# Gated cross-attention block: quantized tokens of blocks 2 to 8 transposed by DMA, with a given order behind the attention and in the first layer

## The chip, the cores and the metric

The kernel runs on one core of a Trainium2 chip. The metric is device time in microseconds of one execution. The time before is 717.9 us, the median of 3 runs (715.8 to 718.52). The profile that is read here is of one execution by itself, with a time of its own.

The engines of the core are TensorE (PE; its weight loads are listed as PEld), VectorE (DVE), ScalarE (ACT), GpSimd (POOL) and SyncE (SP), which here only issues DMAs. SBUF is the on-chip memory that all of them and the DMAs reach; PSUM is the accumulation memory that TensorE writes.

## The reference

A Flamingo-style gated block with x of 2 x 2048 tokens of 512 numbers, and 77 context tokens for each of the 2 batch entries:

```python
x = x + tanh(g_xattn) * xattn(layernorm(x), ctx, ctx, Wq, bq, Wk, bk, Wv, bv, Wo, bo)
x = x + tanh(g_ffn) * ffn(layernorm(x), w1, b1, w2, b2)

def ffn(x, w1, b1, w2, b2):               # 512 -> 2048 -> 512
    h = qlinear(x.reshape(-1, 512), w1, b1)
    h = gelu(h, approximate=False)
    return qlinear(h, w2, b2)

def qlinear(x, w, b):
    xq, sx = quant_per_tensor(x)
    wq, sw = quant_per_tensor(w)
    return (xq @ wq.T + b) * (sw * sx)

def quant_per_tensor(x):
    scale = max(max(abs(x)), 1e-6) / 127
    return round(x / scale), scale
```

The attention has 16 heads of 32. What matters is that each scale is one number for the whole tensor: no token of the first layer can be quantized before the attention is done for all tokens and the largest absolute value of the normalized x is known, and no hidden value can be quantized before the first layer is done for all tokens.

## The kernel before, in words

The 4096 tokens are cut into 8 blocks of 512 (block 1 is index i = 0 in the code, block 8 is i = 7), and a block into 4 tiles of 128 tokens. x stays in SBUF for all blocks. There are three stages.

**Attention.** For each block and each of 8 steps (a group of 4 heads, half of the tokens), TensorE computes scores, VectorE subtracts the maximum, ScalarE takes the exponential, VectorE sums and GpSimd divides; TensorE transposes the probabilities, applies V and projects (L326), and VectorE adds the result to x (L333). Afterwards `norm2_stats` and `norm2_max` compute for each tile the statistics of the second layer norm and the largest absolute value of the normalized tokens (`xmax`). For the last block these follow tile by tile. Weights are quantized on the way.

**Between attention and first layer.** Block 1's tokens are normalized on GpSimd (L529, four instructions), `scale_of` turns `xmax` into the scale `s_x` and its inverse `inv_x` on all partitions (a diagonal, one matmul by ones, a maximum), and `quantize_x` multiplies by it, rounds by adding and subtracting a large constant, and writes the integers as bf16 (`xq`). The first layer needs tokens on the free axis and features on the partitions, so TensorE transposes each tile in four pieces of 128x128 into PSUM (`px`, L553) and ScalarE copies it to `xqT` (L556).

**First layer.** For each block, four G tiles of four chunks of 128 hidden units. A chunk is four accumulating matmuls `ph <- w1q, xqT` (L583) of 128x512. Two chunks share one PSUM tile `ph` (two banks, two such tiles), each of which ScalarE turns into `G` by a Gelu (L590); VectorE takes the maximum of |G| over two chunks (L600). G tiles of the first six blocks are stored to DRAM by SyncE's queue (L611, 1 MB each); those of the last two stay in SBUF (8 buffers in all). While block i is in the matmuls, VectorE normalizes and quantizes block i + 1 (L529, L167, L168), TensorE transposes it and VectorE copies the result (L558). What each engine issues next is chosen by a scheduler that goes by priority, except where `issue_after` puts an instruction behind another one of the same engine, or `manual_schedule` keeps an engine to the order of the source.

**Second layer.** The scale of the hidden values is computed in the same way; G is quantized by ScalarE and VectorE (L636, L637), multiplied by `w2q` (L645), scaled and added to x (L659, L663) and stored. The 24 G tiles in DRAM are loaded again (L630) as buffers come free.

The bias b2 is loaded at the start, by the same queue of SyncE as x and the weights (L118).

The two loops that the change touches, as quoted below with their line numbers:

Of the kernel before, what the change touches and what calls it, by code (L numbers as in the profile page):

```python
# [15 lines left out]
P = 128  # L16
D = 512
# [25 lines left out]
def tile_flamingo_gated_block(  # L43
# [47 lines left out]
    wq_sb = awts.tile([P, KC, D], F32, name="wq_sb")  # L91
    wo_sb = awts.tile([P, KC, D], F32, name="wo_sb")
    ctx_sb = awts.tile([P, B, KC, NK], F32, name="ctx_sb")
    bv_sb = awts.tile([NK, D], F32, name="bv_sb")
    bq_sb = const.tile([P, KC], F32, name="bq_sb")
    bk_sb = const.tile([P, KC], F32, name="bk_sb")
    tg = const.tile([P, 2], F32, name="tg")
    bo_sb = const.tile([P, D], F32, name="bo_sb")
    b1_sb = const.tile([P, FC], F32, name="b1_sb")
    b2_sb = const.tile([P, D], F32, name="b2_sb")  # L100

    load_x(0, pieces=NT)
    nc.scalar.dma_start(bq_sb, bq)
# [11 lines left out]
    nc.sync.dma_start(tg[:, 1:2], g_ffn.to_broadcast([P, 1]))  # L115
    nc.sync.dma_start(bo_sb, bo.to_broadcast([P, D]))
    nc.sync.dma_start(b1_sb, b1)
    nc.sync.dma_start(b2_sb, b2.to_broadcast([P, D]))  # L118

    ident = const.tile([P, P], F32, name="ident")  # L120
    make_identity(nc, ident)
# [5 lines left out]
    nc.gpsimd.memset(mhalf, -0.5)  # L127

    w1q = const.tile([P, KC, FF], BF16, name="w1q")
    w2q = const.tile([P, FC, D], BF16, name="w2q")  # L130
    mean2 = const.tile([P, NB, NT, 2], F32, name="mean2")
    rstd2 = const.tile([P, NB, NT], F32, name="rstd2")
# [15 lines left out]
    def scale_of(maxima, name, psum, tag):  # L148
# [13 lines left out]
        nc.vector.reciprocal(inv, s)  # L162
        return s, inv

    def quantize(dst, src, inv):

        nc.vector.tensor_scalar(src, src, inv, MAGIC, ALU.mult, ALU.add)  # L167
        return nc.vector.tensor_scalar(dst, src, MAGIC, None, ALU.subtract).ins  # L168
# [3 lines left out]

    s_w, inv_w = {}, {}
    with actx:
        work = actx.enter_context(tc.tile_pool(name="work", bufs=2))
        ps_s = actx.enter_context(tc.tile_pool(name="ps_s", bufs=2, space=PSUM))
        ps_t = actx.enter_context(tc.tile_pool(name="ps_t", bufs=2, space=PSUM))
        ps_p = actx.enter_context(tc.tile_pool(name="ps_p", bufs=2, space=PSUM))

        kblk, vblk = [], []  # L180
        for b in range(B):
            kb = awts.tile([P, NG, RK], F32, name=f"kb{b}")
            nc.gpsimd.memset(kb, 0.0)
            kblk.append(kb)
            vblk.append(awts.tile([NK, D], F32, name=f"vb{b}"))

        def project_k(b, g):

# [153 lines left out]
        def norm2_max(i, t0=0, t1=NT):  # L342

            tm = small.tile([P, NT], F32, tag="tm", name=f"tm{i}_{t0}")
            for t in range(t0, t1):
                xn = work.tile([P, D], F32, tag="xn", name=f"xf{i}_{t}")
                nc.vector.tensor_scalar(
                    xn,
                    X[i][:, t, :],
                    mean2[:, i, t, 0:1],  # L350
                    rstd2[:, i, t : t + 1],
                    ALU.subtract,
                    ALU.mult,
                )
                nc.vector.tensor_reduce(
                    tm[:, t - t0 : t - t0 + 1], xn, AX.X, ALU.max, apply_absolute_value=True
                )
            k = i if t1 - t0 == NT else NB - 1 + t0
            nc.vector.tensor_reduce(xmax[:, k : k + 1], tm[:, : t1 - t0], AX.X, ALU.max)

# [65 lines left out]
        for i in range(NB):  # L428
            for s in range(2 * NG):
                last = None  # L430
                if s + 1 < 2 * NG:
                    last = softmax(i, s + 1)
                    last_product = last["POOL"]
                elif i + 1 < NB:
                    last = softmax(i + 1, 0)
                transpose_a(i, s, 0)

                if i == 0 and s < 2:
                    project_k(0, s + 2)
                if s == 0:  # L440
                    if i > 0:
                        apply_v(i - 1, NG - 1)
                    project_q(i, 1)
                if i == 0 and s == 1:
                    project_v(0)
                if i == 0 and s == 2:


                    with tc.issue_after(last["ACT"]):
                        nc.scalar.activation(tg, tg, AF.Tanh)  # L450
                    with tc.issue_after(last["POOL"]):
                        nc.gpsimd.tensor_scalar(bo_sb, bo_sb, tg[:, 0:1], None, ALU.mult)
                if s in (2, 4):
                    project_q(i, 1 + s // 2)
                    apply_v(i, s // 2 - 1)
                if s in (1, 3, 5, 6) and i > 0:
                    project_o(i - 1, (1, 3, 5, 6).index(s))
                if s == 6:
                    apply_v(i, 2)
                if i + 1 < NB:  # L460
                    if s == 3:
                        with tc.issue_after(last["DVE"]):
                            norm(i + 1)
                    if s in (5, 6):
                        for t in (2 * s - 10, 2 * s - 9):
                            transpose_x(i + 1, t)
                transpose_a(i, s, 1)
                if s == 6 and i + 1 < NB:
                    project_q(i + 1, 0)
                if i == 0 and 3 <= s < 7:  # L470
                    for b in range(1, B):
                        project_k(b, s - 3)
                        if s == 6:
                            project_v(b)
                if s == 7 and i > 0:
                    norm2_stats(i - 1)
                    norm2_max(i - 1)
                if last is not None:
                    with tc.issue_after(last["DVE"]):
                        weight_step(i, s)  # L480
                    t = s - NT if i == 0 else s // 2
                    if t >= 0 and (i == 0 or s % 2 == 0):
                        with tc.issue_after(last["POOL"]):
                            add_bias(i, t)
            if i + 2 < NB:
                load_x(i + 2)
            if i == 0:
                load_w("w1", w1_piece, range(4))
            if i == 2:
                load_w("w2", w2_piece, range(2))  # L490
# [4 lines left out]
        for t in range(NT):  # L495
            project_o(NB - 1, t)
            last = norm2_stats(NB - 1, t, t + 1)
            if t > 0:
                with tc.issue_after(last):
                    norm2_max(NB - 1, t - 1, t)  # L500
        norm2_max(NB - 1, NT - 1, NT)
    s_w1, s_w2 = s_w["w1"], s_w["w2"]


# [1 line left out]
    hidden_dram = ctx.enter_context(  # L506
        tc.tile_pool(name="hidden_dram", bufs=1, space=bass.MemoryType.DRAM)
    )

    def gtile(name):  # L510
        return gpool.tile([P, GF, TB], F32, tag="G", name=name)
# [5 lines left out]
    with ExitStack() as fctx:  # L517
# [1 line left out]
        ps_h = fctx.enter_context(  # L519
            tc.tile_pool(name="ps_h", bufs=2, space=PSUM, reuse_waits="tile")  # L520
        )
        ps_x = fctx.enter_context(
            tc.tile_pool(name="ps_x", bufs=2, space=PSUM, reuse_waits="tile")
        )

        def normalize_x(i, engine):
            xs = fwork.tile([P, NT, D], F32, tag="xs", name=f"xs{i}")
            for t in range(NT):
                engine.tensor_scalar(  # L529
                    xs[:, t, :],  # L530
                    X[i][:, t, :],
                    mean2[:, i, t, 0:1],
                    rstd2[:, i, t : t + 1],
                    ALU.subtract,
                    ALU.mult,
                )
            return xs

        def quantize_x(i, xs, n):

            xq = fwork.tile([P, NT, D], BF16, tag="xq", name=f"xq{i}")
            xqT = fwork.tile([P, KC, TB], BF16, tag="xqT", name=f"xqT{i}")
            for t0 in range(0, NT, n):
                v, vq = xs[:, t0 : t0 + n, :], xq[:, t0 : t0 + n, :]
                if n == 1 and t0 >= NT // 2:
                    nc.scalar.activation(v, v, AF.Copy, bias=MAGIC, scale=inv_x)
                    last = nc.vector.tensor_scalar(vq, v, MAGIC, None, ALU.subtract).ins
                else:
                    last = quantize(vq, v, inv_x)
                for t in range(t0, t0 + n):  # L550
                    px = ps_x.tile([P, KC, P], BF16, tag="px", name=f"px{i}_{t}")
                    for kc in range(KC):
                        nc.tensor.transpose(px[:, kc, :], xq[:, t, kc * P : (kc + 1) * P], identb)  # L553
                    dst = xqT[:, :, t * P : (t + 1) * P]
                    if n == 1:
                        nc.scalar.copy(dst, px)  # L556
                    else:
                        nc.vector.tensor_copy(dst, px)  # L558
            return xqT, last


        with tc.issue_after(last_product), tc.high_priority(offset=300):
            xs = normalize_x(0, nc.gpsimd)
        s_x, inv_x = scale_of(xmax, "x", ps_g, "pg")
        xqT, last = quantize_x(0, xs, 1)
        s1 = const.tile([P, 1], F32, name="s1")
        nc.vector.tensor_tensor(s1, s_x, s_w1, ALU.mult)
        b1s = const.tile([P, FC], F32, name="b1s")
        nc.vector.tensor_scalar(b1s, b1_sb, s1, None, ALU.mult)
        for i in range(NB):  # L570
            cur = xqT
            if i + 1 < NB:
                with tc.issue_after(last):
                    xs = normalize_x(i + 1, nc.vector)
                xqT, last = quantize_x(i + 1, xs, NT)
            for a in range(GT):
                G = gtile(f"G{i}_{a}")
                for v in range(GF // 2):
# [149 lines left out]
```

## Time and profile before

| What | us |
|---|---|
| median of 3 runs | 717.9 |
| the profiled execution's own time | 718.17 |
| its span, first to last instruction | 716.2 |
| first matmul of the first layer, after the span's start | 457.57 |
| ScalarE's last Gelu begins | 584.26 |
| first matmul of the second layer | 592.33 |

The page divides the span into 40 equal slices; a digit is the busy share in tenths (9 is 90% or more). PEclk is the clock that TensorE was granted, in tenths, DMA the busy share of 16 DMA engines:

```profile
PE   4998999899999999999999997699999978999977
PEld 2655445445445445454555543344444433444433
DVE  3564678889888799587577668799997669855542
ACT  2455344334344334444444440477777779454540
POOL 2134323234232342432333232300000009991000
PEclk9999999999999999999999999699999999999999
DMA  9900200121311311100000000066666107699871
```

One slice is 17.9 us. The attention ends in slice 25 to 26 (digit 7 and 6 of PE; the granted clock falls to 0.6 there), the first layer follows to the slice with digit 7 after the row of nines, then the second layer.

The groups of instructions that the change touches (line, engine, operation, out<-in, partitions x elements, count | busy us, mean ns of one | idle before it, and what ended it):

```profile
L583 PE MATMUL ph<-xqT,w1q 128*128 128x512 bf16 x512 | 124.2, 381 | 0.9 <-ACT xqT L556 0.7
L590 ACT ACTIVATE G<-ph,b1s,s 128x512 f32<-128x512 f32 x128 | 99.5, 777 | 28.9 <-PE ph L583 23.8
L600 DVE TENSOR_REDUCE hmax<-G 128x1 f32<-128x1024 f32 x63 | 73.9, 1213 | 16.0 <-ACT G L590 15.7
L529 DVE TENSOR_SCALAR xs<-x,mean,rstd 128x512 f32<-128x512 f32 x28 | 14.0, 540 | 0.0
L553 PE MATMUL px<-identb,xq 128*128 128x128 bf16 x128 | 11.6, 230 | 5.1 <-DVE xq L168 2.7 <-ACT xqT L556 2.4
L558 DVE COPY xqT<-px 128x512 bf16<-128x512 bf16 x28 | 10.6, 416 | 1.2 <-PE px L553 1.0
L167 DVE TENSOR_SCALAR xs<-xs,inv_x 128x2048 f32<-128x2048 f32 x7 | 9.0, 1281 | 0.1
L529 POOL TENSOR_SCALAR xs<-x,mean,rstd 128x512 f32<-128x512 f32 x4 | 8.7, 2174 | 0.0
L168 DVE TENSOR_SCALAR xq<-xs 128x2048 bf16<-128x2048 f32 x7 | 8.5, 1218 | 0.0
```

A matmul's mean (381 ns) is from its start to its end in a pipeline, so that neighbours overlap; how many fit into a time is read from when they start.

### The profile page before, as it was taken

To read this page: it belongs to the slowest core of one execution; us is meant where nothing else is said; L and a number is where in the kernel's file an instruction comes from. 1 tells how busy PE (TensorE), PEld (TensorE's weight loads), DVE (VectorE), ACT (ScalarE), POOL (GpSimd) and SP (SyncE) were. 2 spreads that over 40 slices of the span, in tenths; PEclk is the share of its full clock that TensorE was granted. 3 is DMA by queue.
4 is the path that set the end of the run, shared out by engine and by line. 5 is a ranking of instruction groups with operands and counts; after the bars stand their busy time and mean duration, and the time that the engine had idled before them with its cause. 6 is when DMAs were issued, how large, how long until landed. Compare 5 with 4: busy or idle time off the path is not lost.

```text
span 716.2 us, 8398 instructions
## 1 busy us (share of the span) xinstructions
PE 662.0 (92%) x3160; PEld 326.6 (46%) x3160; DVE 526.9 (74%) x821; ACT 345.7 (48%) x474; POOL 210.7 (29%) x164
## 2 busy tenths in 40 slices
PE   4998999899999999999999997699999978999977
PEld 2655445445445445454555543344444433444433
DVE  3564678889888799587577668799997669855542
ACT  2455344334344334444444440477777779454540
POOL 2134323234232342432333232300000009991000
PEclk9999999999999999999999999699999999999999
DMA  9900200121311311100000000066666107699871
GB/s 300 343 1 11 107 0 1 37 82 59 118 59 59 119 59 59 59 1 0 1 1 0 1 1 0 22 271 259 271 265 264 59 0 293 249 346 335 329 253 74
DMA packets 26432, 85.44 MB, mean 119 GB/s; under 512 B 3531, under 2 KB 3531, under 8 KB 20248
## 3 DMA queue, kind: packets, MB, share of 16 engines
q1 hardware_dynamic: 24520, 83.54, 31.0%
q10 hardware_dynamic: 1872, 1.37, 0.6%
q8 instruction: 25, 0.41, 0.2%
q14 instruction: 15, 0.12, 0.0%
HBM read 51.34 MB, written 33.55 MB: 119 GB/s over the span
## 4 chain that ended last, share of the span: by engine, by line
PE 58%; DVE 21%; DMA 7%; POOL 6%; ACT 4%; issue 3%; SPq 1%; POOLq 0%; DVEq 0%; ACTq 0%
PE ph L583 17%; PE pq L248 9%; PE po L326 8%; PE pf L645 7%; PE pta L304 6%; DMA Gb<-h 6%; PE ps L267 4%; POOL e L291 3%; DVE mx L276 3%; PE pc L313 3%; DVE sm L288 2%; DVE e L280 2%; DVE st_a L141 2%; ACT Gb L636 1%; DVE st_f L141 1%
## 5 line engine op out<-in xcount | busy, mean ns | idle before, releaser
L291 POOL TENSOR_TENSOR e<-e,rs 128x616 f32<-128x616 f32 x64 | 77.9, 1218 | 261.7 <-DVE rs L290 190.2
L583 PE MATMUL ph<-xqT,w1q 128*128 128x512 bf16 x512 | 124.2, 381 | 0.9 <-ACT xqT L556 0.7
L645 PE MATMUL pf<-w2q,hq 128*128 128x512 bf16 x512 | 114.4, 386 | 9.4 <-DVE hq L637 4.9
L248 PE MATMUL pq<-xnT,wq_sb 128*128 128x512 f32 x256 | 121.0, 613 | 0.9 <-ACT xnT L240 0.9
L305 ACT COPY aT<-pta 77x512 f32<-77x512 f32 x128 | 73.5, 580 | 93.7 <-PE pta L304 93.6
L326 PE MATMUL po<-wo_sb,cT 128*128 128x512 f32 x256 | 117.5, 597 | 0.0
L590 ACT ACTIVATE G<-ph,b1s,s 128x512 f32<-128x512 f32 x128 | 99.5, 777 | 28.9 <-PE ph L583 23.8
L659 POOL TENSOR_TENSOR x<-x,b_sb 128x512 f32<-128x512 f32 x32 | 57.9, 1853 | 135.6 <-DVE b_sb L616 135.6
L304 PE MATMUL pta<-ident,e 128*77 128x128 f32 x512 | 81.2, 284 | 13.8 <-POOL e L291 11.0
L304 PEld LDWEIGHTS pta<-ident,e 128*77 128x77 f32 x512 | 57.7, 147 | 68.1 <-POOL e L291 33.7
L600 DVE TENSOR_REDUCE hmax<-G 128x1 f32<-128x1024 f32 (+1 forms) x65 | 75.2, 1196 | 16.4 <-ACT G L590 16.1
L645 PEld LDWEIGHTS <-hq 128*128 128x128 bf16 x512 | 50.4, 99 | 73.2 <-issue 8.3
L583 PEld LDWEIGHTS <-w1q 128*128 128x128 bf16 x512 | 49.2, 97 | 67.6 <-issue 18.2
L276 DVE TENSOR_REDUCE mx<-ps 128x8 f32<-128x616 f32 x64 | 50.2, 786 | 39.9 <-PE ps L267 39.6
L248 PEld LDWEIGHTS pq<-xnT,wq_sb 128*128 128x128 f32 x256 | 46.7, 194 | 53.2 <-issue 50.2
L636 ACT ACTIVATE Gb<-Gb,inv_h 128x2048 f32<-128x2048 f32 x24 | 47.6, 1999 | 46.3 <-DMA Gb<-h 46.3
L288 DVE TENSOR_REDUCE sm<-e 128x8 f32<-128x616 f32 x64 | 50.4, 789 | 25.0 <-ACT e L286 24.4
L286 ACT ACTIVATE e<-e 128x616 f32<-128x616 f32 x64 | 45.8, 716 | 42.6 <-DVE e L280 42.5
L326 PEld LDWEIGHTS po<-wo_sb,cT 128*128 128x128 f32 x256 | 45.6, 190 | 45.0 <-issue 44.5
L637 DVE TENSOR_SCALAR hq<-Gb 128x2048 bf16<-128x2048 f32 x24 | 36.9, 1547 | 32.2 <-ACT Gb L636 32.2
L267 PE MATMUL ps<-kb,qT 64*128 64x154 f32 x512 | 55.5, 319 | 0.9 <-ACT qT L256 0.8
L256 ACT ACTIVATE qT<-pq,bq_sb 128x512 f32<-128x512 f32 x32 | 22.0, 687 | 65.5 <-PE pq L248 65.5
(90 smaller groups left out, 646.5 us busy)
## 6 DMA issues: line engine op xcount, KB each, us to landing
h<-G SPq DMA_DIRECT2D x24, 1024.0 KB, 3.8
Gb<-h SPq DMA_DIRECT2D x24, 1024.0 KB, 7.2
raw_w<-in_w2T SPq DMA_DIRECT2D x8, 1024.0 KB, 5.0
out_y<-x SPq DMA_DIRECT2D x32, 256.0 KB, 3.8
x<-in_x SPq DMA_DIRECT2D x7, 1024.0 KB, 5.0
raw_w<-in_w1T SPq DMA_DIRECT2D x4, 1024.0 KB, 9.8
x<-in_x SPq DMA_DIRECT2D x4, 256.0 KB, 6.2
wq_sb<-in_wqT ACTq DMA_DIRECT2D x1, 1024.0 KB, 10.6
```

The source lines that it names most:

```text
L248: nc.tensor.matmul(pq, wq_sb[:, kc, g * P : (g + 1) * P], xnT[i][:, kc, :], start=(kc == 0), stop=(kc == KC - 1),)
L267: nc.tensor.matmul(ps[:, q, u * RK : (u + 1) * RK], qT[i, g][r, t * P : (t + 1) * P], kblk[i // NBB][r, g, :], start=True, stop=True,)
L276: nc.vector.tensor_reduce(mx, sc, AX.X, ALU.max)
L288: nc.vector.tensor_reduce(sm, e4, AX.X, ALU.add)
L291: last["POOL"] = nc.gpsimd.tensor_tensor(e4, e4, rs[:, :, :, None].to_broadcast([P, 2, HG, NK]), ALU.mult).ins
L304: nc.tensor.transpose(pt[:NK, j, :], es[i, s][:, u, j, :], ident)
L305: nc.scalar.copy(aT[i, g][:, :, t * P : (t + 1) * P], pt[:NK, :, :])
L326: nc.tensor.matmul(po, cT[i, g][:, t * P : (t + 1) * P], wo_sb[:, g, :], start=(g == 0), stop=(g == NG - 1),)
L583: nc.tensor.matmul(ph[:, u, :], w1q[:, kc, fc * P : (fc + 1) * P], cur[:, kc, :], start=(kc == 0), stop=(kc == KC - 1),)
L590: nc.scalar.activation(G[:, 2 * v + u, :], ph[:, u, :], AF.Gelu, bias=b1s[:, fc : fc + 1], scale=s1,)
L600: nc.vector.tensor_reduce(hmax[:, k + u : k + u + 1], G[:, 2 * v + u : 2 * v + u + n, :], AX.XY, ALU.max, apply_absolute_value=True,)
L645: nc.tensor.matmul(po[t], hq[:, fc, t * P : (t + 1) * P], w2q[:, fc, :], start=(fc == 0), stop=(fc == FC - 1),)
```

## The change

Four things, all between the end of the attention and the end of the first layer:

- Tokens of blocks 2 to 8 are transposed by `dma_start_transpose` on SyncE's queue, one DMA for each tile of 128 tokens (128x512 bf16, SBUF to SBUF), 28 in all. TensorE's transposes of these blocks, the PSUM tiles for them and the copies go. `xq`, `xqT` and `xs` keep two buffers each.
- The first layer's matmuls are issued by TensorE in the order of the source (`manual_schedule` for PE), so both halves of one `ph` tile come before the next tile.
- Block 1's normalization is done by VectorE in the last step but one of the last block's attention, into a buffer of the attention's pool; its quantization, still by TensorE's transposes, is written out behind the attention: two tiles by VectorE, two by ScalarE and VectorE, the copies from PSUM by ScalarE and VectorE in turn. The maxima of the last block are chained in order.
- Some tiles move: `xqT0` is a tile of its own, `bv_sb` shares a buffer with `cT`, and `b2_sb` is allocated and loaded after the attention. The load stands in SyncE's queue between the last load of x and the first transposing DMA.

In the instruction order of the built program, SyncE's queue has block 2's four transposing DMAs first, then two stores of G, block 3's four, and from block 4 on two ahead of a block's last store and two behind it (block 4's around the last store of block 2, and so on). Each of these waits for the quantized tile, and from block 4 on also for TensorE to have left the block whose buffer it writes.

```diff
-    b2_sb = const.tile([P, D], F32, name="b2_sb")
...
-    nc.sync.dma_start(b2_sb, b2.to_broadcast([P, D]))
...
+    xqT0 = const.tile([P, KC, TB], BF16, name="xqT0")
...
+    def normalize2(dst, i, t):
+        nc.vector.tensor_scalar(
+            dst, X[i][:, t, :], mean2[:, i, t, 0:1], rstd2[:, i, t : t + 1],
+            ALU.subtract, ALU.mult,
+        )
+
+    def transpose_q(dst, src):
+        for kc in range(KC):
+            nc.tensor.transpose(dst[:, kc, :], src[:, kc * P : (kc + 1) * P], identb)
...
                     with tc.issue_after(last["DVE"]):
                         weight_step(i, s)
+                        if i == NB - 1 and s == 6:
+                            xs0 = work.tile([P, NT, D], F32, tag="aT", name="xs0", bufs=3)
+                            for t in range(NT):
+                                normalize2(xs0[:, t, :], 0, t)
...
             if t > 0:
                 with tc.issue_after(last):
-                    norm2_max(NB - 1, t - 1, t)
-        norm2_max(NB - 1, NT - 1, NT)
+                    last = norm2_max(NB - 1, t - 1, t)
+        with tc.issue_after(last):
+            norm2_max(NB - 1, NT - 1, NT)
+        s_x, inv_x = scale_of(xmax, "x", ps_p, "pp")
+        xq0 = work.tile([P, NT, D], BF16, tag="xnT", name="xq0", bufs=1)
+        for t in range(NT):
+            v, vq = xs0[:, t, :], xq0[:, t, :]
+            if t < NT // 2:
+                with tc.issue_after(last):
+                    last = quantize(vq, v, inv_x)
+            else:
+                nc.scalar.activation(v, v, AF.Copy, bias=MAGIC, scale=inv_x)
+                last = nc.vector.tensor_scalar(vq, v, MAGIC, None, ALU.subtract).ins
+        for t in range(NT):
+            px = ps_t.tile([P, KC, P], BF16, tag="pt", name=f"px0_{t}")
+            transpose_q(px, xq0[:, t, :])
+            copy = nc.vector.tensor_copy if t % 2 else nc.scalar.copy
+            copy(xqT0[:, :, t * P : (t + 1) * P], px)
...
+    late = ctx.enter_context(tc.tile_pool(name="late", bufs=1, reuse_waits="tile"))
+    b2_sb = late.tile([P, D], F32, name="b2_sb")
+    nc.sync.dma_start(b2_sb, b2.to_broadcast([P, D]))
...
-        def quantize_x(i, xs, n):
...
-                for t in range(t0, t0 + n):
-                    px = ps_x.tile([P, KC, P], BF16, tag="px", name=f"px{i}_{t}")
-                    for kc in range(KC):
-                        nc.tensor.transpose(px[:, kc, :], xq[:, t, kc * P : (kc + 1) * P], identb)
-                    dst = xqT[:, :, t * P : (t + 1) * P]
-                    if n == 1:
-                        nc.scalar.copy(dst, px)
-                    else:
-                        nc.vector.tensor_copy(dst, px)
-            return xqT, last
...
-        with tc.issue_after(last_product), tc.high_priority(offset=300):
-            xs = normalize_x(0, nc.gpsimd)
-        s_x, inv_x = scale_of(xmax, "x", ps_g, "pg")
-        xqT, last = quantize_x(0, xs, 1)
+        def quantize_x(i):
+            xs = fwork.tile([P, NT, D], F32, tag="xs", name=f"xs{i}")
+            xq = fwork.tile([P, NT, D], BF16, tag="xq", name=f"xq{i}")
+            xqT = fwork.tile([P, KC, TB], BF16, tag="xqT", name=f"xqT{i}")
+            for t in range(NT):
+                normalize2(xs[:, t, :], i, t)
+            quantize(xq, xs, inv_x)
+            for t in range(NT):
+                nc.sync.dma_start_transpose(xqT[:, :, t * P : (t + 1) * P], xq[:, t, :])
+            return xqT
...
+        fctx.enter_context(tc.manual_schedule(engines={mybir.EngineType.PE}))
         for i in range(NB):
-            cur = xqT
+            cur = xqT if i else xqT0
             if i + 1 < NB:
                 with tc.issue_after(last):
-                    xs = normalize_x(i + 1, nc.vector)
-                xqT, last = quantize_x(i + 1, xs, NT)
+                    xqT = quantize_x(i + 1)
```

## The prediction

> **What bounds the kernel now.** I read the page's head first, then the busy times by stage, then the chain of waits inside the stages that the change touches.
>
> ```profile
> span 716.2 us, 8398 instructions
> PE 662.0 (92%) x3160; PEld 326.6 (46%) x3160; DVE 526.9 (74%) x821; ACT 345.7 (48%) x474; POOL 210.7 (29%) x164
> ```
>
> 92% over the whole span says little, because the kernel has three stages. The columns of the next view are: stage, its length, busy us of PE, PEld, DVE, ACT, POOL, granted clock, DMA share, GB/s.
>
> ```profile
> 457.57:584.24 126.67, 126.42 (x621) 55.72 (x621) 109.29 (x130) 97.92 (x126) 0.00 (x0) 0.99 0.49 200
> 429.11:457.57 28.46, 16.91 (x55) 8.22 (x51) 22.20 (x52) 5.54 (x9) 11.54 (x8) 0.81 0.00 0
> ...
> 592.33:716.20 123.87, 112.57 (x508) 49.94 (x508) 73.61 (x63) 58.82 (x30) 55.77 (x31) 0.98 0.74 272
> ```
>
> The first layer (126.67 us) looks like a full TensorE. The 28.46 us before it hold a hole. The second layer is code that the change leaves alone. Its chain repeats "DMA Gb<-h", ACT, DVE, output store from 635 to 697 us, so I let it shift rigidly.
>
> The hole, in the chain of waits (start, us, what):
>
> ```profile
> 443.15 0.76 DVE x L333
> ...
> 445.11 0.78 POOL rstd L145
> 445.89 8.67 POOL xs L529 x4
> 454.56 0.02 issue
> 454.58 0.72 ACT xs L546
> 455.30 0.48 ACT xqT L556
> 455.78 0.04 issue
> 455.82 0.60 PE px L553 x4
> 456.44 1.08 ACT xqT L556 x2
> 457.57 4.02 PE ph L583 x12
> ```
>
> The reader is to see that four GpSimd normalizations of block 1 (8.67 us) set the start of the first layer, although block 1's data was ready hundreds of microseconds earlier. The scale that the quantization needs is there at 450.39, as the timeline shows:
>
> ```profile
> 450.23 0.16 DVE L162 RECIPROCAL inv_x<-s_x 128x1 f32<-128x1 f32 x1
> ```
>
> Inside the first layer, the same chain, and the activations of a nearby stretch:
>
> ```profile
> 487.69 1.89 PE ph L583 x8
> 489.58 1.02 PE ph L583 x4
> 490.60 0.45 PE px L553 x8
> 491.05 1.73 PE ph L583 x8
> ```
>
> ```profile
> 483.07 1.64 ACT L590 ACTIVATE G<-ph,b1s,s 128x512 f32<-128x512 f32 x2 [0.25 <-PE ph L583]
> ...
> 483.91 1.17 PEld L583 LDWEIGHTS <-w1q 128*128 128x128 bf16 x6 [0.29 <-issue]
> 484.97 0.78 ACT L590 ACTIVATE G<-ph,b1s,s 128x512 f32<-128x512 f32 x1 [0.25 <-PE ph L583]
> ```
>
> Eight matmuls take 1.89 us, but only 1.73 right after a transpose has let ScalarE catch up. So TensorE is not full: every eighth matmul loses 0.16 us. The activation of 484.97 ends at 485.75, and the chain's next group starts at 485.79. The instruction order explains it. Before, the scheduler issues A0 B0 A1 B1 C0 (letters are PSUM tiles, digits their halves), and C reuses A's banks. C0 thus waits for the activation of A1, for which only B1's four matmuls (0.86 us) leave time, and the activation (0.78) plus its hand-overs is longer.
>
> **The change part by part.**
>
> (1) First layer's order. In source order, A0 A1 B0 B1 C0, the same wait has eight matmuls (1.73 us) of cover for 0.78 us. What the stalls cost: 512 matmuls by 1.73/8 = 0.216 are 110.6; 112 transposes by 0.45/8 = 0.056 are 6.3; the first six matmuls start 0.43 apart while the clock is low (the stage before has a granted clock of 0.81), 1.3 more. 126.67 - 110.6 - 6.3 - 1.3 = 8.5 us, or 53 stalls of 0.16. I book **-8.5**. ScalarE must sustain two activations per 1.73 us; they take 1.64 as a pair, so it just does.
>
> (2) The 112 TensorE transposes leave TensorE: **-6.3**. Their 28 VectorE copies (10.6 us) leave VectorE too. VectorE's work per block becomes 8 x 1.21 (maxima) + 4 x 0.54 (normalize) + 1.28 + 1.22 (quantize) = 14.3 us beside 13.8 of matmuls (64 x 0.216). It was about 16. So it falls behind by 0.5 us a block, 3.5 in seven; eight G buffers of 3.45 us each cover that, and the last block, with 9.7 us of VectorE work, takes it back. Without cover it would cost 3.5.
>
> (3) In their place 28 DMA transposes of 128x512 bf16 (128 KB), four per block, on SyncE's queue with the 1 MB stores of G. No such operation is in the trace. What it must fit:
>
> ```profile
> 480.00:560.00 80.00, 79.87 (x404) 35.66 (x403) 73.41 (x90) 62.56 (x82) 0.00 (x0) 1.00 0.64 263
> ```
>
> ```profile
> h<-G SPq DMA_DIRECT2D x24, 1024.0 KB, 3.8
> ...
> out_y<-x SPq DMA_DIRECT2D x32, 256.0 KB, 3.8
> ```
>
> 263 GB/s at a share of 0.64 is 411 GB/s of full engines, so a store occupies them 2.55 us, and four 10.2 of a block's 13.8. That leaves 3.6 us, 0.9 for each transpose. Low end: at the stores' rate, 128 KB take 0.32 us. High end: each one is issued only after the last has landed, 3.8 us like a 256 KB output store. Between them: queue 10 moves 1872 packets in 0.6% of 16 engines' span, 37 ns each; a transpose as 512 rows of 256 B costs 512 x 37 / 16 = 1.2 us. I take 0.6 us, between 0.32 and 1.2, since queue and source are the stores' own. Then 10.2 + 2.4 = 12.6 us fit into 13.8, and I book **0**. The cover is one block: tokens of block i+2 go out when TensorE has left block i, and are needed 13.8 us later. In SyncE's queue two stand ahead of block i's last store and two behind it, so a late one delays stores, then G buffers, then ScalarE. The first four have 11 us: block 2's tokens are quantized 5.4 us of VectorE work after the copies, at about 461, and TensorE is in block 1 until about 471. VectorE also waits: quantized tiles have two buffers, so block 6's quantization stands behind block 4's transposes, with the maxima queued behind it, again on the G buffers' slack.
>
> The Trainium skill speaks against this part: VectorE: DVE Perf Modes, "The three transpose paths", gives 390 ns for a 128x128 bf16 transpose on TensorE and 1309 ns by DMA, and its rules prefer TensorE where PSUM will do. The trace's TensorE transposes follow each other at 56 ns, so the table seems to hold isolated times; if its 1309 ns were a rate, a block would need 16 x 1.309 = 20.9 us, and the estimate by that page is (20.9 + 3.8 - 13.8) x 6 = 65 us over my sum. Advanced Engine Details and Errata, "X-Bar Transpose (TRN2)", says instead that transposing DMAs run about as fast as plain ones, which is my low end and gives my sum. No run here shows either yet.
>
> (4) Stage behind the attention. Block 1's normalization moves from GpSimd to VectorE, into the last softmax of block 8: 4 x 0.54 us. Two lie in VectorE's 0.78 us wait for an exponential, one between sum and reciprocal, one after it. The probabilities are 0.75 us later, TensorE's last attention transposes some 0.5 after slack: **+0.5** (bounds 0 and 2.2). The maxima of block 8 are put in strict order, so the scale comes 0.35 earlier. From 450.05 VectorE does s1 0.47, scale 0.47, b1s 0.23, round 0.64, scale 0.47, round 0.54, 0.64: at 453.5 TensorE has tile 2; three tiles of transposes at 0.5 and a copy of 0.43 end at 455.45, where matmuls begin instead of 457.57: **-2.1**. Net -1.6.
>
> (5) The load of b2 (256 KB, 5.9 us to land) goes from the start to SyncE's queue ahead of the first transposes. It is issued once the attention's buffers are free, about 455, and is through before 461: 0. It is read only after the first layer.
>
> Sum: -8.5 - 6.3 - 1.6 = -16.4 against this execution's 716.2: span 699.8. Its own time is 718.17, 1.97 around the span, against a median of 717.9: **702 us**, own range 698 to 706.
>
> **The rivals.**
> (R1, the slower side) The transposes exceed the DMA's room. From 0.9 us each, TensorE waits at every block start of the last six; from 10.2 + 4x = 13.8 + 16.4/6, that is x = 1.6 us, the kernel is slower than before. At the high end a block takes 4 x 3.8 + 3.8 (the store between them) = 19.0 us, 5.2 too many, six times: 702 + 31 = 733. For it: the DMA is already 64% busy, and one queue does it all. Against: two blocks' buffers and neighbouring transfers that overlap now.
> (R2) The same, mildly: 1.2 us each gives 15.0 per block, 1.2 late six times, 709.
> (R3) The order brings nothing, since ScalarE at 1.64 of 1.73 us is too near its limit: 702 + 8.5 = 710.5. Against: its idle before G, 0.25 us in each pair, is all wait for TensorE.
> (R4) VectorE's lag is not covered: 702 + 3.5 = 705.5, inside my range.
>
> **How the numbers follow.** A measurement of this kernel can tell about 0.5% from no change, that is 714.3 to 721.5. Forecast with R4: 0.60. R2 and R3: 0.17. R1: 0.23, of which 0.04 falls within 0.5% and 0.19 above. Range 697 to 719: it leaves out most of R1 and a little below. Faster 0.77, same 0.04, slower 0.19.
>
> **What would show it.** Right: eight matmuls in 1.73 us throughout the first layer, the layer near 112 us, no wait of TensorE for a DMA at block starts, matmuls beginning near 455.5. Wrong: "PE ph" waiting for "DMA xqT" at the start of blocks 3 to 8, stores landing much later than 3.8 us, ScalarE waiting for G buffers. What I know least is the transposes' rate; if the prediction fails badly, it fails there.

## The result, and the profile after

The changed kernel takes 765.62 us (median of 4 runs) against 716.85 us for the one before: ratio 1.067, 95% interval 1.062 to 1.072. The forecast was 702 us, in a range of 697 to 719 us. The time moved the other way.

The span of the changed kernel's profiled execution is 764.4 us. Its stages (columns as before):

```profile
453.05:634.64 181.59, 125.14 (x512) 50.44 (x512) 105.92 (x107) 99.47 (x128) 0.00 (x0) 0.97 0.45 159
428.00:453.05 25.05, 16.99 (x54) 8.00 (x50) 20.50 (x53) 4.58 (x7) 2.88 (x4) 0.88 0.00 0
...
641.00:764.40 123.40, 114.20 (x508) 50.27 (x508) 75.17 (x64) 58.91 (x31) 55.80 (x31) 0.97 0.74 273
```

The reader is to see one stage that has changed for the worse. The first layer, from its first matmul to the last Gelu's end, is 181.6 us; in the trace before it was 128.3 (457.57 to 585.90). (The last Gelu before begins at 585.13, not at 584.26 as the table ahead has it, where a pair of Gelus begins; four matmuls of the second layer run at 589.96 already, ahead of its 592.33.) TensorE is busy 125 us of the layer, about as before, and idle for the rest. The first layer begins 4.5 us earlier, and the second layer (123.4 us) only shifts. The layer's 53.3 us more, less these 4.5, are 48.8 us, against 48.2 us between the two spans.

The cycle that the first layer repeats, in the chain of waits of the changed kernel:

```profile
500.60 1.90 PE ph L583 x8
502.50 0.03 issue
502.53 0.79 ACT G L590
503.31 0.04 issue
503.36 1.90 PE ph L583 x8
```

Before, this chain held TensorE alone, in groups of 1.89 us. Now eight matmuls, one Gelu, and eight matmuls again: 2.75 us each time (503.36 - 500.60 = 2.76), and 64 x 2.75 = 176 of the layer's 181.6 us. Each group of eight is followed by a Gelu, whose end releases the next group. The list of groups says so in one line, with the releaser of the idle time at its end (the line before had 0.9 us of idle there, for another reason):

```profile
L583 PE MATMUL ph<-xqT,w1q 128*128 128x512 bf16 x512 | 125.1, 388 | 56.1 <-ACT G L590 55.6
```

What the prediction feared did not happen. The transposing DMAs, by the two views that name them (nanoseconds min/median/max of SyncE's issue, then us to landing), and the waits of the stage (us in total, times, longest):

```profile
L563 SPq DMA_TRANSPOSE xqT<-xq x28: 1201/1282/2161, 458.2 to 595.0; - x28
...
DMA to landing us min/median/max: 2.4/2.5/4.6
```

```profile
PE ph L583 <- ACT G L590: 55.6, 64, 0.9
DVE xq L185 <- DMA xqT<-xq: 2.1, 3, 0.8
```

No matmul waits for a DMA; VectorE does three times, for 2.1 us in all. The wait for ScalarE comes 64 times, once for each PSUM tile of two halves. Its place within the tile shows at the start of the stage (start, us, engine, what, count, idle time before it and its releaser):

```profile
453.05 1.89 PE L583 MATMUL ph<-xqT,w1q 128*128 128x512 bf16 x4 [0.52 <-DVE xqT L528]
454.98 0.78 ACT L590 ACTIVATE G<-ph,b1s,s 128x512 f32<-128x512 f32 x1 [2.50 <-PE ph L583]
455.81 3.57 PE L583 MATMUL ph<-xqT,w1q 128*128 128x512 bf16 x8 [0.87 <-ACT G L590]
```

The first four matmuls fill the first half of the layer's first tile. The fifth, which opens the second half, starts only when the first Gelu is done. In that tile no earlier contents can be meant. It is the Gelu that reads the tile's own first half, in another bank.

### The profile page after: what moved, and what is told of

It reads as the page before. It is cut to its first block, busy times and chain, and to the rows that moved or that the text cites. A ratio compares the mean times of both kernels' runs of the same rounds, so it can differ in the third digit from the quotient of the medians.

```text
span 764.4 us, 8199 instructions
## 1 busy us (share of the span) xinstructions
PE 660.4 (86%) x3048; PEld 320.9 (42%) x3048; DVE 522.9 (68%) x799; ACT 344.7 (45%) x472; POOL 202.0 (26%) x160
## 4 chain that ended last, share of the span: by engine, by line
PE 53%; DVE 21%; ACT 10%; DMA 7%; POOL 4%; issue 3%; SPq 0%; POOLq 0%; DVEq 0%; ACTq 0%
PE ph L583 16%; PE pq L260 9%; PE po L338 8%; ACT G L590 7%; DMA Gb<-h 7%; PE pta L316 6%; PE pf L645 6%; PE ps L279 4%; POOL e L303 3%; DVE mx L288 3%; DVE sm L300 2%; PE pc L325 2%; DVE st_a L143 2%; DVE e L292 2%; ACT Gb L636 2%
## 5 line engine op out<-in xcount | busy, mean ns | idle before, releaser
L583 PE MATMUL ph<-xqT,w1q 128*128 128x512 bf16 x512 | 125.1, 388 | 56.1 <-ACT G L590 55.6
L600 DVE TENSOR_REDUCE hmax<-G 128x1 f32<-128x1024 f32 (+1 forms) x65 | 78.1, 1202 | 73.5 <-ACT G L590 73.3
L645 PE MATMUL pf<-w2q,hq 128*128 128x512 bf16 x512 | 116.1, 390 | 7.8 <-DVE hq L637 5.0
L583 PEld LDWEIGHTS <-w1q 128*128 128x128 bf16 x512 | 50.4, 99 | 130.6 <-issue 78.9
L316 PEld LDWEIGHTS pta<-ident,e 128*77 128x77 f32 x512 | 57.7, 147 | 68.2 <-POOL e L303 34.2
L292 DVE TENSOR_TENSOR e<-ps,mx 128x616 f32<-128x616 f32 x64 | 50.9, 797 | 3.3 <-POOL e L303 0.5
```

The source lines that it names most:

```text
L292: last["DVE"] = nc.vector.tensor_tensor(e.rearrange("p u (q r k) -> p q u r k", q=NR, r=RT), sc, mx[:, :, :, :, None].to_broadcast([P, NR, ...
L316: nc.tensor.transpose(pt[:NK, j, :], es[i, s][:, u, j, :], ident)
L583: nc.tensor.matmul(ph[:, u, :], w1q[:, kc, fc * P : (fc + 1) * P], cur[:, kc, :], start=(kc == 0), stop=(kc == KC - 1),)
L600: nc.vector.tensor_reduce(hmax[:, k + u : k + u + 1], G[:, 2 * v + u : 2 * v + u + n, :], AX.XY, ALU.max, apply_absolute_value=True,)
L645: nc.tensor.matmul(po[t], hq[:, fc, t * P : (t + 1) * P], w2q[:, fc, :], start=(fc == 0), stop=(fc == FC - 1),)
```

## The experiments

The theory after this first reading (A): a write into the second half of a two-bank `ph` tile waits for ScalarE's read of its first half. In the source's order A0 A1 B0 B1, TensorE stands still from A0's end to the end of A0's Gelu. Its rivals: the DMA transposes or SyncE's queue set the pace, or they would at a faster one.

Times are medians; the layer is from its first matmul to the last Gelu's end, in the profiled execution. Each ratio of e1 to e11 is to runs of the kernel before made beside that version (medians 718.2 us for e1 to e4, 719.15 for e5 and e6, 718.92 for e10 and e11), not to 716.85.

| Kernel | time, us | ratio to before (95%) | first layer, us |
|---|---|---|---|
| before | 716.85 | 1 | 128.3 |
| changed | 765.62 | 1.067 (1.062 to 1.072) | 181.6 |
| e1 changed, one-bank tiles | 698.02 | 0.971 (0.966 to 0.976) | 114.0 |
| e2 changed, scheduler's order | 708.92 | 0.988 (0.983 to 0.992) | 123.9 |
| e3 before, one-bank tiles | 711.25 | 0.990 (0.988 to 0.993) | 123.1 |
| e4 before, DMA transposes | 709.08 | 0.988 (0.984 to 0.993) | 124.3 |
| e5 before, new stage | 751.0 | 1.045 (1.041 to 1.048) | 165.7 |
| e6 one-bank tiles, new stage, TensorE transposes | 706.69 | 0.983 (0.981 to 0.986) | 122.5 |
| e8 as e1, DMA transposes doubled | 733.12 (one run) | | 149.8 |
| e9 before, order of the source | 773.26 (one run) | | 185.8 |
| e10 as e1, old stage | 701.02 | 0.977 (0.973 to 0.980) | 114.0 |
| e11 as e1, again | 697.59 | 0.972 (0.969 to 0.974) | 113.8 |

### e1: a PSUM tile for each half

```diff
-            tc.tile_pool(name="ps_h", bufs=2, space=PSUM, reuse_waits="tile")
+            tc.tile_pool(name="ps_h", bufs=4, space=PSUM, reuse_waits="tile")
...
-                    ph = ps_h.tile([P, 2, TB], F32, tag="ph", name=f"ph{i}_{a}_{v}")
                     for u in range(2):
                         fc = a * GF + 2 * v + u
+                        ph = ps_h.tile([P, TB], F32, tag="ph", name=f"ph{i}_{a}_{v}_{u}")
```

(and `ph` for `ph[:, u, :]` in the matmul and the Gelu)

> The changed kernel, but each chunk of 128 hidden units gets a PSUM tile of its own (one bank, four tiles) in place of one half of a two-bank tile (two tiles); order of the source kept. Theory A (in source order the second half of a tile waits for ScalarE to read the first half of the same tile, so TensorE and ScalarE take turns: 1.90 + 0.16 + 0.79 = 2.75 us per eight matmuls): the wait disappears, eight matmuls take 1.73 us, the first layer falls from 181.6 to about 113 us, the time to about 698 us. Rival B (the transposing DMAs or SyncE's queue set the pace and the wait for ScalarE only follows): the layer stays above 150 us, the time above 735 us. Rival C (DMAs fit at 22 us a block but not at 14 us): the layer comes to 120 to 135 us with TensorE waiting for xqT at block starts, time 705 to 720 us.

Measured: 698.02 us, and a layer of 114.0 us. As many banks, the same order, the same work; only the tile's borders moved, and 67.6 us went. (The expectation's three terms add up to 2.85; the chain's own are 1.90 + 0.03 + 0.79 + 0.04 = 2.76.) The chain of waits of e1:

```profile
467.18 10.74 PE ph L583 x49
477.92 0.05 issue
477.97 10.74 PE ph L583 x49
```

TensorE alone, without a break. (Each line of x49 stands for 50 matmuls: a record is missing after every 49, 501 of 512 are there. 10.79 us by 50 is 0.216. In e11, the same kernel with all 512 on record, the chain holds the layer's matmuls in one piece, 453.28 111.22 PE ph L583 x504.) Theory A holds, rivals B and C fall. This version is 2.9% faster than the kernel before.

### e2: the changed kernel with the scheduler's order

```diff
-        fctx.enter_context(tc.manual_schedule(engines={mybir.EngineType.PE}))
```

> The changed kernel with TensorE's order in the first layer left to the scheduler again (which alternates the halves of two tiles: A0 B0 A1 B1); two-bank tiles, DMA transposes and the stage behind the attention kept. Theory A: between A0 and A1 lie B0's four matmuls, so each pair of halves loses 0.16 us only: 110.6 + 1.3 + 64 x 0.165 + 0.8 = 123 us for the layer, time about 708 us. Rival B (DMAs set the pace): no gain against the changed kernel, above 750 us.

Measured: 708.92 us, layer 123.9 us. One line of the change, taken back, returns 56.7 us. Its chain shows the old cycle:

```profile
506.29 1.89 PE ph L582 x8
508.18 0.00 issue
508.18 1.89 PE ph L582 x8
```

### e3: the kernel before with one-bank tiles

The edit of e1, in the kernel before.

> The kernel before with one-bank PSUM tiles (four) for the chunks; nothing else. Theory A (the 0.16 us lost by every eighth matmul before is the same wait, half covered): 53 stalls go, -8.5 us, time about 708 us. Rival (the stall before is the reuse of a tile's banks two tiles later, as the prediction had it; the same four banks are reused after as many matmuls): no change, 717 us.

Measured: 711.25 us, a gain of 1.0% (0.7 to 1.2) where 8.5 us, 1.2%, was expected. The stall of 0.16 us in every eighth matmul is gone with the shared tile. This alone doesn't part theory A from the rival: with one-bank tiles a reuse, too, waits for the one Gelu of its own bank, with twelve matmuls of cover, so the rival's "no change" does not follow from it. The first tiles of the trace before part them (see (1) below). The layer gained 5.2 us; the 3 us missing to 8.5 are in gaps just ahead of TensorE's own transposes, which the scheduler places where they wait for VectorE.

### e4: the kernel before with DMA transposes alone

```diff
                 for t in range(t0, t0 + n):
+                    if n > 1:
+                        nc.sync.dma_start_transpose(xqT[:, :, t * P : (t + 1) * P], xq[:, t, :])
+                        continue
```

> The kernel before with the transposes of blocks 2 to 8 by DMA and nothing else (order by the scheduler, block 1 as before). Theory A (the DMA transposes are hidden): 112 transposes leave TensorE (-6.3 us), but the stalls that they covered come back (11 more of 0.165, +1.8): about 712.5 us. Rival B (DMA transposes cost): TensorE waits for xqT at block starts, above 720 us.

Measured: 709.08 us, 1.2% faster (0.7 to 1.6). The transposes by DMA were no loss. The layer of 124.3 us is near the 123.8 that theory A gives (128.3 - 4.5); a second layer that was 6 us shorter in the profiled execution than before (120.2 against 126.2 us from its first matmul) flatters the rest.

### e5: the kernel before with the new stage alone

The changed kernel with the order left to the scheduler and the transposes of blocks 2 to 8 given back to TensorE, through two PSUM tiles and copies by VectorE as before.

> The kernel before with only the stage behind the attention changed (block 1 normalized on VectorE during the last softmax, chained maxima, copies shared; room in SBUF as in the changed kernel); blocks 2 to 8 transposed by TensorE, order by the scheduler, two-bank tiles. From the changed kernel's trace (first matmul of the first layer at 453.05 instead of 457.57): -4.5 us, about 713 us; the prediction's own step would give -1.6, about 715 us. Rival (the earlier start came with the DMA transposes or the order): no change, 717 us.

A miss: 751.0 us, and not by the stage, which is 11.1 us long as in the changed kernel. The layer is 165.7 us. The scheduler chose another order here, from TensorE's first transposes in the layer on; why, the runs don't show. By the waits and signals of the matmuls in the trace it is three matmuls of the next tile's first half, then the second half of the tile before, then the fourth matmul of the first half. The chain of waits:

```profile
502.56 1.71 PE ph L588 x7
504.27 0.03 issue
504.30 0.79 ACT G L595
```

2.56 us from a Gelu's end to the next one's, eight matmuls (1.71 + 0.03 + 0.79 + 0.04; the eighth starts in front of the seven that the chain lists). Now two Gelus, 0.79 each, lie between the first half's last matmul and the second half's first, with only three matmuls (0.65 us) to cover them. The wait between halves accounts for the cycle, but not alone: the matmul that is released behind the Gelu of 504.30 opens a new tile, so the reuse of a tile binds there as well. With one-bank tiles this kernel takes 706.7 us (e6). The experiment failed as a measure of the stage (e10 does that) and shows how fragile the order before was.

### e6: one-bank tiles, new stage, TensorE's transposes

e5 with the edit of e1.

> One-bank tiles and the new stage behind the attention, but the transposes of blocks 2 to 8 on TensorE (with the copies on VectorE) and TensorE's order by the scheduler: tells what the DMA transposes are worth where no wait between halves hides it. Theory A (hidden DMA transposes against 6.3 us of TensorE, and the waits that TensorE's transposes meet, 3 us more than booked in the one-bank version of the kernel before): 698 + 6 to 9 = 704 to 707 us. Rival (the DMA transposes, at 90% of the DMA in that version, cost as much as they save): 698 us.

Measured: 706.69 us, as expected, 8.7 us more than e1. So where no wait between halves hides it, moving the transposes to the DMAs is worth 8.7 us: 6.3 of TensorE's time and some 2 of waits around it. (e6 also leaves TensorE's order to the scheduler; e10 does so with DMA transposes and has e1's layer of 114.0 us, so the order is not what costs here.)

### e8: every transposing DMA twice

```diff
                 nc.sync.dma_start_transpose(xqT[:, :, t * P : (t + 1) * P], xq[:, t, :])
+                spare = fwork.tile([P, KC, P], BF16, tag="spare", name=f"sp{i}_{t}", bufs=3)
+                nc.sync.dma_start_transpose(spare, xq[:, t, :])
```

> The one-bank version of the changed kernel with every transposing DMA issued twice, the second into a spare tile that nobody reads (28 more, 128 KB each). In that version a transpose keeps the 16 engines 0.77 us (512 packets of 256 B) and the DMA is 90% busy from 470 to 560 us. If the DMA's room is the limit: 10.5 + 8 x 0.77 = 16.7 us against 13.8 a block, six times 2.9: about 715 us, with TensorE waiting for xqT at block starts. If the transposes only have latency to hide: 698 us. If SyncE's issue time of 2.15 us each is the limit: 8 x 2.15 + 1.3 = 18.5 us a block, about 726 us.

Measured: 733.12 us. The prediction's rival R1, brought about on purpose:

```profile
PE ph L585 <- DMA xqT<-xq: 24.4, 6, 5.8
```

Matmuls wait for a block's tokens, up to 5.8 us at a time, and the granted clock is lower (0.91 from 455 to 585 us, against 0.98 over e1's layer). The one run is 18 us above the 715 us of the DMA's bare time and 7 us above the 726 us of the issue time. Which of the two decides isn't settled: the issues here took 1.27 us at the median, not 2.15, and VectorE waits for the second transposes too (6.8 us in two waits), since they read its tiles.

### e9: the kernel before in the order of the source

```diff
+        fctx.enter_context(tc.manual_schedule(engines={mybir.EngineType.PE}))
         for i in range(NB):
...
+                if i + 1 < NB and a >= 2:
+                    for t in (2 * a - 4, 2 * a - 3):
...
```

(TensorE's transposes of the next block stand ahead of its third and fourth G tile.)

> The kernel before with TensorE kept to the order of the source in the first layer (both halves of a two-bank tile one after the other) and nothing else of the change; TensorE's transposes of the next block stand in the middle of a block. Theory A (the order alone makes the loss): 64 x 2.75 + 6.3 + some waits for copies = 184 to 192 us for the layer instead of 128, time 772 to 782 us. Rival (it takes the DMA transposes or the queue to lose): below 725 us.

Measured: 773.26 us, layer 185.8 us. The order alone, without DMA transposes and without the new stage, makes the whole loss (one run, but 54 us from the kernel before) and repeats the cycle:

```profile
555.47 0.79 ACT G L601
556.26 0.04 issue
556.30 1.90 PE ph L594 x8
```

### e10 and e11: what the stage behind the attention is worth

e10 is e4 with the edit of e1; e11 is e1 again, beside it.

> The one-bank version of the changed kernel without the new stage behind the attention and without the moved load of b2 (that is, the kernel before with one-bank tiles and DMA transposes; TensorE's instruction order of the matmuls is the same). The traces put the stage at 14.46 us before and 11.09 us after, from the attention's last matmul to the first layer's first: if that is kept to the end, this kernel is 3.4 us slower than the one-bank version, about 701.5 us. If the second layer gives it back (it has its own 3 us of scatter), no difference, 698 us.

> The one-bank version of the changed kernel once more, beside the last one, for an interval fine enough to tell 3.4 us: 698 us again.

Measured: 701.02 against 697.59 us, 3.4 us apart as the traces say. The two intervals (0.973 to 0.980 and 0.969 to 0.974) just touch, so this rests on the traces as much as on the times: from the attention's last matmul to the first layer's first, 14.46 us in e10, 11.00 us in e11.

## Why the prediction was wrong, point by point

**(1) The first layer's order: the step that failed.** It booked -8.5 us; the order cost 57.5 us in the layer (185.8 in e9 against 128.3 before; the changed kernel against e2 gives 57.7). The prediction had seen the stall of 0.16 us and that the Gelu ending at 485.75 released the group of 485.79. It then named the wrong wait: "C reuses A's banks. C0 thus waits for the activation of A1". What it left out is A1's wait for A0's Gelu. Both waits fit the timing of the order A0 B0 A1 B1: either way there is one Gelu to wait for and four matmuls of cover. They part in the order A0 A1 B0 B1: reuse then has eight matmuls of cover, a wait between halves has none. What tells them apart stood in the trace before, in the first two tiles, where nothing was there to be reused:

```profile
460.76 0.78 ACT L590 ACTIVATE G<-ph,b1s,s 128x512 f32<-128x512 f32 x1 [0.51 <-PE ph L583]
461.59 0.38 PE L583 MATMUL ph<-xqT,w1q 128*128 128x512 bf16 x1
```

The first row is B0's Gelu, which ends at 461.54. The second is the layer's 13th matmul, the first of B1: it starts 0.38 us after the 12th in place of 0.22, just behind that Gelu. Counted on from there, the group of 485.79 starts with the 109th matmul, which is again a second half's first and not a C0, if the scheduler kept to the order A0 B0 A1 B1 throughout. Of the 56 such stalls in that trace (9.4 us; the prediction had 53 and 8.5), 32 then fall on a second half and 24 on the start of a new tile: the wait that the prediction named exists too, but was not the only one. By theory A the step would have been 64 x (2.75 - 1.89) = +55 us. e1, e2 and e9 show it from three sides.

**(2) TensorE's transposes.** Booked -6.3. Shown by e6 against e1 as 8.7, since they also cost waits: the size was a little low. In the changed kernel VectorE was free for long stretches, so that its lag could not matter.

**(3) The transposing DMAs.** Booked 0, and 0 it was: no matmul waits for one in the changed kernel nor, at full speed, in e1. In the changed kernel the engines' share of 0.58 over 80 us, less 15 stores at 2.55 us, leaves an estimate of 0.7 us for each of 12 transposes. Summed over the trace's packets, 512 of 256 B for each transpose, it is 0.63 us of the 16 engines (0.77 in e1); 0.6 had been assumed, so this was rightly sized. Block 2's transposes were issued from 458.2 on, where the prediction had about 461. At the pace of e1 it is close:

```profile
470.00:560.00 90.00, 89.58 (x411) 40.79 (x418) 82.40 (x84) 81.03 (x105) 0.00 (x0) 1.00 0.90 298
```

```profile
h<-G SPq DMA_DIRECT2D x21, 1024.0 KB, 6.1
xqT<-xq SPq DMA_TRANSPOSE x24, 5.0
```

The first is e1's stretch with the DMAs busy 90%, the second its issues with the us to landing: stores 6.1 instead of 3.8, transposes 5.0 instead of 2.5. It all still fits under one block of matmuls, and e8 shows that twice as many do not. R1 was the right mechanism for another kernel. The Trainium skill's 1309 ns per 128x128 (VectorE: DVE Perf Modes, "The three transpose paths") is no rate here, as a tile of four such transposes was on the engines for about 0.63 us. The statement of Advanced Engine Details and Errata ("X-Bar Transpose (TRN2)") that transposing DMAs are as fast as regular ones comes nearer, though 0.63 is still twice the 0.32 us that the prediction estimated for a plain store of the same bytes.

**(4) The stage behind the attention.** Booked -1.6, measured -3.4 (14.46 to 11.09 us). The mechanism was right and VectorE's prices were too high. The end of the chain in the changed kernel:

```profile
449.70 0.39 DVE xs L184
450.10 0.34 DVE xq L523
450.43 0.35 DVE xq L185
450.78 0.05 issue
450.83 0.62 PE px L180 x4
```

A rounding takes 422 ns by its group's mean (0.33 to its successor's start), where 636 and 538 ns were taken from before. From the scale (448.71) to the last rounding that TensorE waits for (450.78) VectorE took 2.07 us, where the prediction added up 3.46; the transposes and copies behind it took 2.27, where it had 1.95. The attention's delay of 0.5 us didn't show: its last matmul ends between 440.9 and 444.5 us in all these profiles, and with the new stage rather earlier than with the old one (medians 442.0 and 443.1).

**(5) b2's load.** Booked 0, and 0 it was: the load is issued at 411.6 us, not at about 455 as the prediction had it, and nothing waits for it.

**The rivals.** R3 said "the order brings nothing" and priced it at 710.5: nearest to the truth in place, but on another ground, ScalarE's own pace, which e1 shows to suffice; and it could only lose the gain. R4's lag of VectorE does not show: in e1 its maxima wait for ScalarE (11.4 us in 22 waits). A slower kernel was given 0.19, all of it to the DMAs (R1), and the transposes' rate was named as the place of a bad failure; no rival let the order itself cost time.

## What to carry to other kernels

A stall that the present order half covers has to be traced to its wait, instruction by instruction, before the order is touched: two explanations that cost the same now may part in the new order, here into -8.5 and +55 us. The first pass through a ring of buffers is the place to look, because there no reuse can be the reason. Give each part that two engines hand over separately a tile of its own; e1's version, with tiles cut that way, is the fastest here at 698 us. With such tiles the layer is also 114.0 us with the order left to the scheduler (e10); other orders were not tried.

## What the runs showed of the hardware that was not expected

- A VectorE rounding of 128x512 (float32 to bf16) took 636 ns before, while GpSimd normalized beside it, and 422 ns with GpSimd idle. Within the kernel before, one took 0.65 us beside it and one 0.43 us after its last instruction had ended.
- A transposing DMA of 128x512 bf16 costs SyncE 1.28 us for each issue at the median (a plain 1 MB store 0.32), and 2.15 us in e1, where the DMAs are 90% busy. In e8, with the DMAs 86% busy, it was 1.27 us, so what sets the issue's time is not shown.
- Why a write into one bank of a tile is made to wait for a read of its other bank was not settled. Four separate tiles in the same number of banks run without the wait, which speaks for the program's tracking of tiles and against a need of the hardware; taking the wait out of a two-bank tile was not tried, so this stays open.
